# Attention over 48x48 pixels: the softmax sums by 32x32 transposes and row sums instead of matrix products with ones

## The chip, the cores and the metric

One core of a Trainium2 chip. The metric is the device time of one execution in microseconds (us), as a median of several. Engines are named as the profile names them: PE (TensorE), DVE (VectorE), ACT (ScalarE), POOL (GpSimd) and SP (SyncE, which only issues DMAs here). A POOL instruction or a DMA that SP issues runs beside the others; each engine takes its own instructions strictly in order.

## What is computed

Four images of 512 channels and 48x48 = 2304 pixels: group norm over 32 groups, a projection to q, k and v, attention in 8 heads of 64 channels over all pixels, an output projection, and the input added to it.

```python
b, c, hh, ww = x.shape                       # 4, 512, 48, 48
t = hh * ww
d = c // num_heads
hn = _group_norm(x, gn_scale, gn_bias)
qkv = jnp.einsum('oc,bchw->bohw', qkv_w, hn) + qkv_b[None, :, None, None]
qkv = qkv.reshape(b, 3, num_heads, d, t).astype(jnp.float16)
q, k, v = (qkv[:, 0], qkv[:, 1], qkv[:, 2])
scale = jnp.asarray(1.0 / math.sqrt(math.sqrt(d)), dtype=jnp.float16)
w = jnp.einsum('bhct,bhcs->bhts', q * scale, k * scale)
w = jax.nn.softmax(w, axis=-1)
a = jnp.einsum('bhts,bhcs->bhct', w, v).astype(jnp.float32)
out = jnp.einsum('oc,bchw->bohw', proj_w, a.reshape(b, c, hh, ww)) + proj_b[None, :, None, None]
return x + out
```

The softmax needs, for each head and each query pixel, the sum of the exponentials over the 2304 key pixels. The kernel takes the exponentials without subtracting a maximum; it checks afterwards that all sums lie between 256 and 60000, and a slower general path behind a branch runs if one doesn't.

## The kernel before, in words

**Tiling.** The heads are worked on in pairs: 4 images by 4 pairs make 16 groups g. The 2304 queries of a pair are cut into five blocks j, four of 512 and one of 256 queries. A block is worked through in *units*: in one unit PE makes scores for three tiles (`BURST`) of 128 keys by 512 queries by two heads (for the narrow block, two tiles of keys by 256 queries take the place of each), and ACT exponentiates them. A wide block has six units, the narrow one three, a pair 27, the whole stream 432. Keys lie on the partitions, queries along the free dimension.

**One unit.** `scores` (L943) writes three double banks `ps` in PSUM (a pool of three, so a unit uses all of them) and ACT makes three exponentials of 128x1024 from them into `p` (L962), a 16-bit tile from a pool of three. `values` (L965) runs two units behind (`BEHIND = 2`): it multiplies the exponentials with v into the one accumulation bank `av` (L980); after the block's last unit the bank is copied out to `avx` (L989). `add` (L991) runs one unit behind on DVE: it adds the unit's `p` to a running 16-bit sum `acc` of 128x3072 (L1009). The first addition of a block takes the `p` of its first two units, so the first unit's `p` is held until then. After the last unit two more additions of 128x1024 join the three parts of `acc` (L1012).

**From `acc` to the result.** `acc` holds, for each of 128 partitions (keys), 2x512 partial sums. `add_up` (L1015) sums over the partitions on PE, by products with a matrix of ones, into a bank `sl` of the same one-bank pool as `av`; every row of `sl` is the sum. `rows` (L1043) copies it to SBUF on DVE and sends one row per head by DMA to `sums`, spread over 128 partitions; `check_sums` (L1063) compares it with the limits on POOL; `invert` (L1073) takes the reciprocal and writes it to a DRAM row; `spread` (L1084) reads that row back, broadcast over 64 partitions per head, as `ib`; `divide` (L1094) multiplies `avx` by `ib` on POOL. These steps lie in successive units.

**Work beside.** PE also makes q and k (L709), v (L760) and the output projection (L844), in chains that share one PSUM bank `pw`; DVE copies each finished chain out (L719, L768, L871), and only then can the next chain start. These chains are cut into pieces that stand in a list `beside`; `fill(n)` issues in each unit n as many as a credit, counted in units, allows. DVE's statistics and normalization of the next image are `tasks`, let in by `fill` with a `room` in us that is smaller near the end of a block.

**The order.** It is written out by hand; no scheduler changes it. The loop at L1350 issues, for each unit n: the sums of the block that ended three units ago (`add_up`, `rows`), `scores(n)`, `add` for unit n-1, `values` for unit n-2, `check_sums` and `invert` for the block that ended four units ago, `spread` (five), `divide` (six), and `fill(n)`; in the unit with the sums `fill(n)` comes before `values`, so that PE has work while DVE empties `sl`. The last two blocks but one of the stream (`soon`) and the last one go by ways of their own.

Of the kernel before, what the change touches and what calls it, by code (L numbers as in the profile page):

```python
# [26 lines left out]
P = 128  # L27
# [5 lines left out]
BURST = 3  # L33
# [434 lines left out]
def fast_path(  # L468
# [13 lines left out]

    RES = NC
# [93 lines left out]
    fine = const.tile([P, 2 * QB // P], F32, name="fine")  # L577
    nc.gpsimd.memset(fine, 1.0)
# [20 lines left out]
    SQ = 32  # L599
# [332 lines left out]
    open_sums = set()  # L932
# [10 lines left out]
    def scores(u):  # L943
        g, j, k, _ = u
        o, n = QBLOCKS[j]
        per = QB // n
        qt, kt = qk[g]
        pt = ppool.tile([P, BURST, 2, QB], F16, tag="p", name=f"p_{g}_{j}_{k}")
        for r in range(BURST):
            ps = ps_s.tile([P, 2, QB], F32, tag="ps", name=f"ps_{g}_{j}_{k}_{r}")  # L950
            for a in range(per):
                i = (k * BURST + r) * per + a
                for h in range(2):
                    rows = slice(h * D, (h + 1) * D)
                    nc.tensor.matmul(  # L955
                        ps[:, h, a * n : (a + 1) * n],
                        kt[rows, bass.ts(i, P)],
                        qt[rows, o : o + n],
                        start=True,
                        stop=True,  # L960
                    )
            nc.scalar.activation(pt[:, r], ps, AF.Exp)  # L962
        pts[u] = pt

    def values(u):  # L965
# [21 lines left out]
        if last and u is not stream[-1]:  # L987
            avx[g, j] = work.tile([P, QB], F32, tag="avx", name=f"avx_{g}_{j}")
            nc.vector.tensor_copy(avx[g, j][:, :n], av[0][:, :n])  # L989

    def add(u):  # L991
# [18 lines left out]
        if last:  # L1010
            for r in range(1, BURST):
                nc.vector.tensor_tensor(t[:, 0], t[:, 0], t[:, r], ALU.add)  # L1012
            acc[g, j] = [t[:, :1]]

    def add_up(g, j, bank=None, more=False):  # L1015
# [5 lines left out]
        if bank is None:  # L1021
# [4 lines left out]
            for r in range(t.shape[1])  # L1026
# [17 lines left out]
    def rows(g, j, sl):  # L1044

        o, n = QBLOCKS[j]
        sx = work.tile([P, QB], F32, tag="rows", name=f"slx_{g}_{j}")
        nc.vector.tensor_copy(sx[:, :n], sl[:, :n])  # L1048
        sm = small.tile([P, 2, QB // P], F32, tag="sums", name=f"sums_{g}_{j}")
        for h in range(2):  # L1050
            nc.sync.dma_start(sm[:, h, : n // P], sx[h * D : h * D + 1, :n])
        sums[g, j] = sm
        return sx

# [107 lines left out]
    def ready(b, j):  # L1162

        if b < B - 1:
            return BEHIND + 6
        return BEHIND + (4 if j == NQ - 3 else 5)
# [139 lines left out]
    def fill(n):  # L1306
# [5 lines left out]
        if ended(n - 1):  # L1312
            room = 1.1 if idle else 0.0
        elif ended(n - BEHIND - 1):
# [40 lines left out]
    for n in range(end):  # L1355
# [3 lines left out]
        summed = block_at(n - BEHIND - 1)  # L1359
        if summed:  # L1360
            rows(*summed, add_up(*summed))
        wanted(stream[n][0])
        scores(stream[n])
        if n > 0:
            add(stream[n - 1])
        if summed:

            fill(n)
        if n >= BEHIND:
            values(stream[n - BEHIND])  # L1370
        if block_at(n - BEHIND - 2):
            check_sums(*block_at(n - BEHIND - 2))
            invert(*block_at(n - BEHIND - 2))
        if block_at(n - BEHIND - 3):
            spread(*block_at(n - BEHIND - 3))
        if block_at(n - BEHIND - 4):

            divide(*block_at(n - BEHIND - 4))
        if not summed:
            fill(n)  # L1380
# [53 lines left out]
    every = fine.shape[1] + n  # L1434
    fines = work.tile([P, QB], F32, tag="rows", name="fines")[:, :every]
    nc.gpsimd.tensor_scalar(fines[:, :n], inv, 1.0 / SUM_MAX, None, ALU.is_ge)
    ok = work.tile([P, QB], F32, tag="avx", name="ok")[:, :n]
    nc.gpsimd.tensor_scalar(ok, inv, 1.0 / SUM_MIN, None, ALU.is_le)
    nc.gpsimd.tensor_tensor(fines[:, :n], fines[:, :n], ok, ALU.mult)
    nc.gpsimd.tensor_copy(fines[:, n:], fine)  # L1440
# [11 lines left out]
    for i, (evacuate, store) in enumerate(ends_of):  # L1452
        if i == NC:
            nc.vector.tensor_reduce(good, fines, AX.X, ALU.add)  # L1454
# [62 lines left out]
```

## Time and profile before

| | |
|---|---|
| Median of 3 runs | 1613.72 us (1612.02 to 1614.79) |
| The profiled execution: its time / its span | 1614.36 us / 1612.6 us |
| Mean granted TensorE clock | 0.996 |
| Busy: PE, ACT, DVE, POOL | 98%, 79%, 71%, 20% |
| Exponentials (L962), 1296 of 1027 ns | 1234.2 us busy |
| Running sums (L1009), 270 of 1809 ns and 79 of 1749 ns | 626.5 us busy |

The page shows one execution: the span runs from its first to its last instruction. A matmul's busy time overlaps the next one's, so a busy PE is read from the distance between starts and not from the sum of durations. In the timelines below a line gives the start, the time covered, the engine, the line of the kernel, the operation with what it writes and reads, how many instructions are merged (x6), and in brackets the engine's idle time before and what ended it.

### The profile page before, as it was taken

Reading aid. Unit: us, or ns where it says so; the run is one execution under the profiler, and the core shown is the slowest. Engines: PE = TensorE matmul, PEld = TensorE weight load, DVE = VectorE, ACT = ScalarE, POOL = GpSimd, SP = SyncE. Lnnn points to the kernel's source line nnn. Section 1 sums busy time; section 2 is a strip of 40 time slices with the busy share of each in tenths; the row PEclk is TensorE's granted clock in tenths of the full one; section 3 lists DMA queues with packets and bytes.
Section 4 is the critical chain, followed back from the end, with each engine's and each line's share of the span. In section 5 each row is a group of like instructions: output and inputs, shape, how many; then the busy total and the mean of one; then the engine's idle time right before and its main releaser. Section 6 shows DMA issues by size and latency. Waiting matters only on the chain. (4 is left out here: it accounts for less than half of the span.)

```text
span 1612.6 us, 28321 instructions
## 1 busy us (share of the span) xinstructions
PE 1583.4 (98%) x11500; PEld 695.7 (43%) x11500; DVE 1140.2 (71%) x1301; ACT 1268.4 (79%) x1361; POOL 319.4 (20%) x458
## 2 busy tenths in 40 slices
PE   7999999999999999999999999999999999999997
PEld 2533434443333534555333353355533334434554
DVE  6167668866666678986666666788666676667775
ACT  3077777888888888888887888887878888888894
POOL 1001112211121222312111121221212131222222
PEclk9999999999999999999999999999999999999998
DMA  6002020100000023511000002352100000016424
GB/s 212 11 14 67 11 66 22 18 14 11 14 18 14 11 67 119 162 46 30 14 9 18 14 12 63 96 154 80 31 14 11 15 15 18 10 29 183 129 60 133
DMA packets 94897, 82.10 MB, mean 51 GB/s; under 512 B 50853, under 2 KB 60965, under 8 KB 94757
## 3 DMA queue, kind: packets, MB, share of 16 engines
q1 hardware_dynamic: 92724, 78.35, 17.8%
q8 instruction: 92, 1.51, 0.4%
q10 hardware_dynamic: 1904, 1.84, 0.4%
q14 instruction: 49, 0.39, 0.1%
q0 software_dynamic: 128, 0.01, 0.0%
HBM read 60.70 MB, written 19.17 MB: 50 GB/s over the span
## 5 line engine op out<-in xcount | busy, mean ns | idle before, releaser
L962 ACT ACTIVATE p<-ps 128x1024 f16<-128x1024 f32 x1296 | 1234.2, 1027 | 310.7 <-PE ps L955 309.6
L1009 DVE TENSOR_TENSOR acc<-acc,p 128x3072 f16<-128x3072 f16 x270 | 488.3, 1809 | 69.8 <-ACT p L962 69.1
L709 PE MATMUL pqk<-x,wqkv 128*64 128x512 f32 (+1 forms) x2464 | 519.3, 551 | 0.0
L980 PE MATMUL av<-p,v 128*64 128x512 f16 (+1 forms) x2880 | 361.1, 364 | 0.4 <-DVE slx L1048 0.3
L955 PE MATMUL ps<-q,k 64*128 64x512 f16 (+1 forms) x2880 | 356.5, 358 | 1.7 <-ACT p L962 1.4
L760 PE MATMUL pv<-wqkv,x 128*64 128x256 f32 x2304 | 268.6, 380 | 0.0
L709 PEld LDWEIGHTS pqk<-x,wqkv 128*64 128x64 f32 x2464 | 168.8, 137 | 224.4 <-issue 166.8
L1070 POOL TENSOR_SCALAR in<-sums 128x8 f32<-128x8 f32 (+1 forms) x158 | 118.4, 749 | 713.3 <-DMA sums<-slx 706.8
L955 PEld LDWEIGHTS <-k 64*128 64x128 f16 x2880 | 106.3, 94 | 277.6 <-issue 228.7
L980 PEld LDWEIGHTS <-v 128*64 128x64 f16 x2880 | 131.9, 109 | 213.0 <-issue 168.8
L1096 POOL TENSOR_TENSOR att<-avx,ib 128x512 f16<-128x512 f32 (+1 forms) x78 | 117.2, 1502 | 451.1 <-DMA ib<-row 424.8
L760 PEld LDWEIGHTS pv<-wqkv,x 128*64 128x64 f32 x2304 | 160.1, 137 | 92.8 <-issue 4.5
L1009 DVE TENSOR_TENSOR acc<-p,p 128x3072 f16<-128x3072 f16 x79 | 138.2, 1749 | 0.0
L844 PE MATMUL pr<-a,whi 128*128 128x512 f32 (+1 forms) x311 | 122.7, 402 | 4.9 <-DVE q L719 2.3
L1012 DVE TENSOR_TENSOR acc<-acc 128x1024 f16<-128x1024 f16 x156 | 111.8, 716 | 5.4
L844 PE MATMUL pr<-a,wlo 128*128 128x512 f32 (+1 forms) x311 | 114.3, 375 | 0.0
L719 DVE TENSOR_SCALAR q<-pqk,bqkv 128x512 f16<-128x512 f32 (+1 forms) x79 | 54.9, 695 | 80.0 <-PE pqk L709 79.8
L719 DVE TENSOR_SCALAR k<-pqk,bqkv 128x512 f16<-128x512 f32 (+1 forms) x75 | 52.2, 696 | 77.9 <-PE pqk L709 77.9
L768 DVE TENSOR_TENSOR v<-pv,bv 128x512 f16<-128x512 f32 x72 | 49.8, 691 | 80.9 <-PE pv L760 80.8
L989 DVE COPY avx<-av 128x512 f32<-128x512 f32 (+1 forms) x79 | 50.6, 641 | 63.7 <-PE av L980 63.6
L871 DVE SCALAR_TENSOR_TENSOR r<-pr,bproj,r 128x512 f32<-128x512 f32 (+1 forms) x80 | 54.9, 695 | 45.2 <-PE pr L844 44.7
L844 PEld LDWEIGHTS pr<-a,whi 128*128 128x128 f32 x311 | 58.7, 189 | 44.1 <-issue 20.2
(69 smaller groups left out, 456.7 us busy)
## 6 DMA issues: line engine op xcount, KB each, us to landing
r<-x_dram SPq DMA_DIRECT2D x72, 256.0 KB, 3.2
out_dram<-r SPq DMA_DIRECT2D x69, 256.0 KB, 2.2
ib<-row SPq DMA_DIRECT2D x126, 128.0 KB, 3.1
x<-x_dram SPq DMA_DIRECT2D x62, 256.0 KB, 4.1
x<-x_dram SPq DMA_DIRECT2D x16, 128.0 KB, 4.8
sums<-slx SPq DMA_DIRECT2D x128, 2.0 KB, 2.1
ib<-row SPq DMA_DIRECT2D x30, 64.0 KB, 3.1
wqkv<-qkv_wT_dram SPq DMA_DIRECT2D x2, 768.0 KB, 6.9
```

The source lines that it names most:

```text
L709: nc.tensor.matmul(pw[0][lo : lo + D, :n], wqkv[:, c, w0 + lo : w0 + lo + D], hn[b, c, j], start=(c == 0), stop=(c == NC - 1),)
L719: nc.vector.tensor_scalar(qk[g][part][:, o : o + n], pw[0][:, :n], bqkv[:, col : col + 1], SCALE, ALU.add, ALU.mult,)
L760: nc.tensor.matmul(pw[0][lo : lo + D, a, :], hn[b, c, i * P // QB][:, at + lo : at + lo + D], wqkv[:, c, 2 * C + half * C // 2 :][:, : C / ...
L844: nc.tensor.matmul(ps[:, :n], w[:, c, bass.ts(m, P)], at32[b, j, c], start=(i == 0), stop=(i == len(steps) - 1),)
L871: nc.vector.scalar_tensor_tensor(xt[:, i], places[i], bias, xt[:, i], ALU.add, ALU.add)
L955: nc.tensor.matmul(ps[:, h, a * n : (a + 1) * n], kt[rows, bass.ts(i, P)], qt[rows, o : o + n], start=True, stop=True,)
L962: nc.scalar.activation(pt[:, r], ps, AF.Exp)
L980: nc.tensor.matmul(av[0][lo : lo + D, :n], vv[b, pr // 2][:, i, pr % 2 * P + lo : pr % 2 * P + lo + D], pt[:, r, h, a * n : (a + 1) * n], ...
L1009: nc.vector.tensor_tensor(t, before, pt, ALU.add)
L1012: nc.vector.tensor_tensor(t[:, 0], t[:, 0], t[:, r], ALU.add)
L1070: nc.gpsimd.tensor_scalar(t, sm, limit, None, op)
L1096: nc.gpsimd.tensor_tensor(atts[g][:, o : o + n], avx.pop((g, j))[:, :n], ibs.pop((g, j))[:, :n], ALU.mult,)
```

## The change

The sums over the partitions leave PE. After the block's last addition DVE joins one of the two remaining parts and POOL the other (128x1024 each). One unit later `turn` transposes the joined 128x1024 on DVE in squares of 32x32, into a part of `acc` that is free by then; one more unit later `fold` sums each run of 32 along the free dimension on DVE, which leaves 128x32 partial sums, one for each of four groups of 32 keys, and sends the four groups by four DMAs side by side onto 32 partitions (`quarters`). `invert_turned`, two units later, adds the four, takes the reciprocal, transposes the 32x32 result back, writes it by two DMAs to the DRAM row, and does the check of the limits on POOL on 32 partitions. `spread` and `divide` follow as before, one unit later than before each, and what uses the result is set one unit later as well (`ready`). Blocks that end near the end of the last pair (`soon` and the last) keep the products with ones, and both joins on DVE.

The copy of `av` to `avx` moves from DVE to ACT. It stands between the second and the third exponential of the unit (`last_exp`). `fill` always comes after `values` now, and its `room` for DVE tasks is cut in the unit of the turning and in that of the inversion.

```diff
@@ -574,8 +575,12 @@
     nc.gpsimd.memset(ones16, 1.0)
-    fine = const.tile([P, 2 * QB // P], F32, name="fine")
-    nc.gpsimd.memset(fine, 1.0)
+    fines = const.tile([P, 2 * QB // P + SQ], F32, name="fine")
+    fine = fines[:, : 2 * QB // P]
+    fine_turned = fines[:SQ, 2 * QB // P :]
+    nc.gpsimd.memset(fines, 1.0)
+    tinv = const.tile([SQ, SQ], F32, name="tinv")
+    nc.gpsimd.memset(tinv, 1.0)
...
@@ -929,7 +933,8 @@
         tc.mark_branch_hint_location("fallback", taken, engines)
-    open_sums = set()
+    open_sums, joined = set(), set()
+    turned = {}
     av, acc, pts, avx, sums, rowd, ibs = {}, {}, {}, {}, {}, {}, {}
...
@@ -959,8 +964,11 @@
                         stop=True,
                     )
-            nc.scalar.activation(pt[:, r], ps, AF.Exp)
+            exp = lambda r=r, ps=ps: nc.scalar.activation(pt[:, r], ps, AF.Exp)
+            if r < BURST - 1:
+                exp()
         pts[u] = pt
+        return exp
...
@@ -986,7 +994,11 @@
         if last and u is not stream[-1]:
             avx[g, j] = work.tile([P, QB], F32, tag="avx", name=f"avx_{g}_{j}")
-            nc.vector.tensor_copy(avx[g, j][:, :n], av[0][:, :n])
+            nc.scalar.copy(avx[g, j][:, :n], av[0][:, :n])
+
+    def by_turning(g, j):
+
+        return g < NG - 1 or j < NQ - 3
...
@@ -1008,9 +1020,11 @@
         nc.vector.tensor_tensor(t, before, pt, ALU.add)
         if last:
+            shared = by_turning(g, j)
             for r in range(1, BURST):
-                nc.vector.tensor_tensor(t[:, 0], t[:, 0], t[:, r], ALU.add)
-            acc[g, j] = [t[:, :1]]
+                engine = nc.gpsimd if shared and r == BURST - 1 else nc.vector
+                engine.tensor_tensor(t[:, 0], t[:, 0], t[:, r], ALU.add)
+            joined.add((g, j))
...
@@ -1023,7 +1037,7 @@
             (t, r, a)
             for t in acc.pop((g, j))
-            for r in range(t.shape[1])
+            for r in range(1 if (g, j) in joined else t.shape[1])
             for a in range(per)
...
@@ -1052,6 +1066,53 @@
         return sx
+    def turn(g, j):
+
+        t = acc.pop((g, j))[0]
+        turned[g, j] = t[:, 1].rearrange("p h n -> p (h n)")
+        nc.vector.transpose(turned[g, j], t[:, 0].rearrange("p h n -> p (h n)"))
+
+    def fold(g, j):
+
+        part = small.tile([P, SQ], F32, tag="part", name=f"part_{g}_{j}")
+        nc.vector.tensor_reduce(
+            part,
+            turned.pop((g, j)).rearrange("p (c k) -> p c k", k=SQ),
+            AX.X,
+            ALU.add,
+        )
+        quarters = small.tile([SQ, P // SQ, SQ], F32, tag="quarters", name=f"qs_{g}_{j}")
+        for p in range(P // SQ):
+            nc.sync.dma_start(quarters[:, p, :], part[bass.ts(p, SQ), :])
+        sums[g, j] = quarters
+
+    def invert_turned(g, j):
+        n = QBLOCKS[j][1]
+        per, cols = QB // n, n // SQ
+        quarters = sums.pop((g, j))
+        sm = small.tile([SQ, 2, cols], F32, tag="tsum", name=f"tsum_{g}_{j}")
+        nc.vector.tensor_reduce(
+            sm,
+            quarters.rearrange("i p (h a c) -> i h c p a", h=2, a=per),
+            AX.XY,
+            ALU.add,
+        )
+        nc.vector.reciprocal(tinv[:, : 2 * cols], sm.rearrange("i h c -> i (h c)"))
+        back = small.tile([SQ, SQ], F32, tag="tback", name=f"tback_{g}_{j}")
+        nc.vector.transpose(back, tinv)
+        row = dram.tile([2, QB], F32, tag="row", name=f"row_{g}_{j}")
+        for h in range(2):
+            nc.sync.dma_start(
+                row[h, :n].rearrange("(c i) -> c i", i=SQ),
+                back[h * cols : (h + 1) * cols, :],
+            )
+        rowd[g, j] = row
+        ok = fine_turned[:, : 2 * cols].rearrange("p (h c) -> p h c", h=2)
+        for op, limit in ((ALU.is_ge, SUM_MIN), (ALU.is_le, SUM_MAX)):
+            t = small.tile([SQ, 2, cols], F32, tag="tin", name=f"tin_{g}_{j}")
+            nc.gpsimd.tensor_scalar(t, sm, limit, None, op)
+            nc.gpsimd.tensor_tensor(ok, ok, t, ALU.mult)
+
     def divide_here(g, j, source, products, engine):
...
@@ -1162,8 +1223,8 @@
         if b < B - 1:
-            return BEHIND + 6
-        return BEHIND + (4 if j == NQ - 3 else 5)
+            return BEHIND + 7
+        return BEHIND + (4 if j == NQ - 3 else 6)
...
@@ -1309,9 +1370,9 @@
         idle = beside and beside[0][4] and not beside[0][4]()
-        if ended(n - 1):
+        if ended(n - 1) or ended(n - BEHIND - 3):
             room = 1.1 if idle else 0.0
-        elif ended(n - BEHIND - 1):
+        elif ended(n - BEHIND):
             room = 1.1 if idle else 0.5
...
@@ -1356,28 +1417,25 @@
         while loads and loads[0][0] <= n:
             loads.popleft()[1]()
-        summed = block_at(n - BEHIND - 1)
-        if summed:
-            rows(*summed, add_up(*summed))
+        if block_at(n - BEHIND - 1):
+            fold(*block_at(n - BEHIND - 1))
         wanted(stream[n][0])
-        scores(stream[n])
+        last_exp = scores(stream[n])
         if n > 0:
             add(stream[n - 1])
-        if summed:
-
-            fill(n)
         if n >= BEHIND:
             values(stream[n - BEHIND])
-        if block_at(n - BEHIND - 2):
-            check_sums(*block_at(n - BEHIND - 2))
-            invert(*block_at(n - BEHIND - 2))
+        last_exp()
+        if block_at(n - BEHIND):
+            turn(*block_at(n - BEHIND))
         if block_at(n - BEHIND - 3):
-            spread(*block_at(n - BEHIND - 3))
+            invert_turned(*block_at(n - BEHIND - 3))
         if block_at(n - BEHIND - 4):
-
-            divide(*block_at(n - BEHIND - 4))
-        if not summed:
-            fill(n)
+            spread(*block_at(n - BEHIND - 4))
+        if block_at(n - BEHIND - 5):
+
+            divide(*block_at(n - BEHIND - 5))
+        fill(n)
         if n - BEHIND in soon:
```

The hunks left out move the definition of `SQ = 32`, and make the final count of checked values cover the added columns of `fines`.

More of the change, by code (lines that the diff above doesn't have):

```diff
@@ L481, in fast_path @@
     nc = tc.nc
+    SQ = 32
     RES = NC
@@ L594, in fast_path @@
     ALL = range(NC)
-    SQ = 32
     NGROUP = SQ // GROUP
@@ L1432, in fast_path @@
     store()
-    every = fine.shape[1] + n
-    fines = work.tile([P, QB], F32, tag="rows", name="fines")[:, :every]
-    nc.gpsimd.tensor_scalar(fines[:, :n], inv, 1.0 / SUM_MAX, None, ALU.is_ge)
+    every = fines.shape[1] + n
+    found = work.tile([P, QB], F32, tag="rows", name="fines")[:, :every]
+    nc.gpsimd.tensor_scalar(found[:, :n], inv, 1.0 / SUM_MAX, None, ALU.is_ge)
     ok = work.tile([P, QB], F32, tag="avx", name="ok")[:, :n]
     nc.gpsimd.tensor_scalar(ok, inv, 1.0 / SUM_MIN, None, ALU.is_le)
-    nc.gpsimd.tensor_tensor(fines[:, :n], fines[:, :n], ok, ALU.mult)
-    nc.gpsimd.tensor_copy(fines[:, n:], fine)
+    nc.gpsimd.tensor_tensor(found[:, :n], found[:, :n], ok, ALU.mult)
+    nc.gpsimd.tensor_copy(found[:, n:], fines)
     expect_end(kinds.Pool)
@@ L1453, in fast_path @@
         if i == NC:
-            nc.vector.tensor_reduce(good, fines, AX.X, ALU.add)
+            nc.vector.tensor_reduce(good, found, AX.X, ALU.add)
             nc.tensor.matmul(pf, good, ones, start=True, stop=True)
```

## Prediction, made before the changed kernel was run

> **What bounds the kernel now.** I read the page's shares first, then the waits, then one block of the stream engine by engine.
>
> ```profile
> PE 1583.4 (98%) x11500; PEld 695.7 (43%) x11500; DVE 1140.2 (71%) x1301; ACT 1268.4 (79%) x1361; POOL 319.4 (20%) x458
> ```
> ```profile
> ACT p L962 <- PE ps L955: 309.6, 404, 46.1
> DVE acc L1009 <- ACT p L962: 69.1, 87, 1.4
> ```
> ```profile
> L955 PE MATMUL ps<-q,k 64*128 64x512 f16 x2304 | 316.7, 380 | 1.7 <-ACT p L962 1.4 <-DVE v L768 0.3
> L1012 DVE TENSOR_TENSOR acc<-acc 128x1024 f16<-128x1024 f16 x156 | 111.8, 716 | 5.4
> L1439 POOL TENSOR_TENSOR fines<-fines,ok 128x256 f32<-128x256 f32 x1 | 0.7, 740 | 0.1
> L1431 POOL TENSOR_TENSOR r<-beyond,r 128x512 f32<-128x512 f32 x1 | 1.3, 1272 | 3.5 <-ACT beyond L1429 3.5
> L1429 ACT COPY beyond<-held 128x512 f32<-128x512 f32 x1 | 0.6, 587 | 3.4 <-PE held L844 3.4
> ```
>
> ACT waits for PE's scores 404 times; PE waits for ACT 1.4 us in all. So PE sets the pace: time leaves PE's program one for one, and PE must not start to wait. The timelines of PE, ACT and DVE at the end of one wide block show how near it is to waiting.
>
> ```profile
> 432.06 0.82 PE L955 MATMUL ps<-q,k 64*128 64x512 f16 x6
> 435.30 0.82 PE L955 MATMUL ps<-q,k 64*128 64x512 f16 x6
> 438.44 0.38 PE L1032 MATMUL sl<-acc,ones 128*64 128x512 f16 x2
> 438.76 0.82 PE L955 MATMUL ps<-q,k 64*128 64x512 f16 x6
> 442.02 0.82 PE L955 MATMUL ps<-q,k 64*128 64x512 f16 x6
> ```
> ```profile
> 435.73 2.86 ACT L962 ACTIVATE p<-ps 128x1024 f16<-128x1024 f32 x3 [0.38 <-PE ps L955]
> 439.19 2.86 ACT L962 ACTIVATE p<-ps 128x1024 f16<-128x1024 f32 x3 [0.60 <-PE ps L955]
> 442.46 2.86 ACT L962 ACTIVATE p<-ps 128x1024 f16<-128x1024 f32 x3 [0.41 <-PE ps L955]
> ```
> ```profile
> 434.36 1.42 DVE L1012 TENSOR_TENSOR acc<-acc 128x1024 f16<-128x1024 f16 x2
> 437.00 0.69 DVE L989 COPY avx<-av 128x512 f32<-128x512 f32 x1 [1.22 <-PE av L980]
> 438.66 0.75 DVE L719 TENSOR_SCALAR q<-pqk,bqkv 128x512 f16<-128x512 f32 x1 [0.97 <-PE pqk L709]
> 439.33 0.68 DVE L1048 COPY slx<-sl 128x512 f32<-128x512 f32 x1
> 439.92 1.75 DVE L1009 TENSOR_TENSOR acc<-p,p 128x3072 f16<-128x3072 f16 x1
> ```
>
> A unit is 3.24 us on PE (432.06 to 435.30), with ACT at work for 2.86 of it: ACT's slack is 0.38. Many units are such *tight* ones; others hold two pieces of beside work and last about 5 us.
>
> **What the Trainium skill says.** "Perfetto Trace Analysis", Identifying the Most-Contended Engine, warns that matmul busy time misleads because matmuls are pipelined; the trace agrees (380 ns each, yet six scores in 0.82), so I use distances between starts. "VectorE: DVE Perf Modes", The three transpose paths: DVE transposes 32x32 squares only, 311 ns for 128x128 of 16 bits. "Vector Engine (DVE) Microarchitecture Reference", The reshape front-end and per-opcode configuration: one element per cycle and lane. The trace has only small transposes, and they agree (128x64 in 246 ns). "GPSIMD Engine Reference", Specifications: POOL shares SBUF interfaces with DVE and contends with its two-input instructions. The trace agrees: beside POOL's product at 639.19 DVE's addition at 639.52 took 2.56 us instead of 1.75.
>
> **The change part by part.** 77 blocks go the new way, 62 wide and 15 narrow.
>
> *PE: the products with ones go.* The unit that holds them takes 3.46 us (435.30 to 438.76), 0.22 over 3.24, and the next 3.26, where the pieces stand in another order. That is 0.24 a wide block. At a narrow one exponentials start 3.40 apart (467.20 to 470.60) and then 3.27: 0.19. Saved: 62 x 0.24 + 15 x 0.19 = 17.7 us. What is issued beside is counted in units, not in time, so PE's program loses these 184 products and little else.
>
> *ACT: the copy of av.* The copy of L1429, the same shape from PSUM, took 587 ns; instructions in a row overlap by 0.1 on ACT (three exponentials of 1.03 in 2.86), so it pushes the third exponential back by 0.48. The last exponential would end at 435.73 + 2.86 + 0.48 = 439.07. PE's next scores start at 438.54 without the sums, their third pair 0.44 later, at 438.98, and it needs the bank that this exponential frees; with 0.05 for the hand-over PE stands still for 0.14. A narrow copy (some 0.3) fits in the slack. From the starts of exponentials, 48 of the wide blocks are tight there: 48 x 0.14 = 6.7 us. Bounds: 0 (the copy hidden) and 0.3 each, 14 us. ACT regains 0.38 in each later unit. The copy frees av before the next block's first product, two thirds of a unit later.
>
> *DVE and POOL: the new chain.* Off DVE go avx 0.69, slx 0.68, one join 0.72, a small reciprocal 0.2: 2.3 us. New are the transpose, 311 + 896/0.96 = 1244 ns (estimate from the page named; range 1.0 to 2.2, the upper end if 16-bit data went at half rate); the row sum of 1024, from 428 ns for 264 elements (L1454), 428 + 760/0.96 = 1.22 us; and for the inversion a sum of 128 elements, a reciprocal of 32 and a 32x32 transpose, some 0.3 + 0.35 + 0.2. That is 3.3, so DVE gains 1.0 x 77 = 77 us, to 76%. The share is harmless; the order matters. POOL's join has no row of its shape: from 740 ns for 256 and 1272 for 512 elements, 2.08 ns each, 1024 take 1272 + 1065 = 2.34 us. It can't be a gain, since DVE's transpose waits for it; bounds 1.3 (16-bit twice as fast) and 3.3 (beside DVE's additions).
>
> In the block shown: first join done 434.36 + 0.72 = 435.08; POOL 435.16 to 437.50; transpose 437.54 to 438.78. Queued behind it is the copy-out of q, ready at 438.66: 438.78 to 439.53. PE's next chain needs that at about 438.67 + 1.42 = 440.1 (scores and values come first), so it holds. Row sum to 440.75, first addition of the next block to 442.50. That addition frees the `p` that the unit at 442.02 fills: its first exponential, at 442.46 before, would now start at 442.46 - 0.22 + 0.14 = 442.38. It starts 0.17 late; PE waits only from 0.35 late on. So the cover has 0.2 us left, and nothing is lost. Where the copy-out falls ahead of the transpose (the order alternates, as chains have two pieces), the chain ends 0.7 earlier. In DVE's order in the changed kernel, a normalization or a statistic (0.55 to 0.65) stands between transpose and copy-out in four tight blocks, and the first block joins 1.1 late: 4 x 0.5 + 1 = 3 us lost.
>
> *Queues.* SP issues eight DMAs for a block instead of five, about 0.55 each (two `ib` took 1.11): 1.7 us more in some 20, behind which only loads stand. POOL's check keeps four instructions on fewer partitions. The result comes one unit later; its readers are set later too, so I count that at nothing; if the cover at the end failed it would be one unit, 3.2 us.
>
> Sum: 1613.7 - 17.7 + 6.7 + 3 = 1605.7. It is against the profiled execution, 1614.36 (span 1612.6 and 1.8 around it); the median is 0.6 lower, and I start from the median.
>
> **The rivals.**
> *A. The chain overshoots (slower).* POOL's join, transpose and row sum are 4.8 us in a row, with 0.2 to spare. Each 0.1 over costs PE 0.1 in about 20 tight blocks whose copy-out comes after the transpose, and half that in as many more. For it: POOL's products in this kernel average 1640 ns instead of 1272, through DVE's additions. Against: DVE mostly waits idle while POOL joins. It decides from 0.5 over. With POOL at 3.3 and the transpose at 1.5, 1.2 over, less 0.2: 1.0 x 20 + 0.5 x 20 = 30 us: 1636. At the mid, 0.5 over net, 15 us: 1621.
> *B. The copy eats the gain (about the same).* If it delays the exponential by 0.6 with its wait for av, and the chain overshoots by 0.2, PE loses 48 x 0.26 + 4 = 16, and 3 for the tasks: 1613.7 - 17.7 + 19 = 1615. For: slack is 0.38 and the copy 0.48 or more. Against: values end well before ACT gets there.
> *C. All of it is hidden:* 1613.7 - 17.7 = 1596. For: DVE idles in every unit. Against: the copy alone is longer than the slack.
> That PE would not lose its products can't be: they are out of the program.
>
> **How the numbers follow.** Forecast (1600 to 1610) 0.45; C 0.10; B 0.18; A 0.27, mostly near 1621. The range takes in C's end and A's middle: 1596 to 1625. A measurement here tells about 0.2%, 3.2 us, from no change: faster means below 1610.5 and slower above 1617. Faster is the forecast and C, 0.55; B lies in between, 0.17 same; A and B's upper edge 0.28.
>
> **What would show it.** Right: units at block ends of 3.24 without the 0.22; PE's waits for ACT at L955 (1.4 now) up to about 7 to 10 us, most just after the copy; POOL's join near 2.3; transpose near 1.25, row sum 1.2; ACT's first exponential three units into a block late by under 0.35. Wrong: POOL's join over 3, a transpose near 2, exponentials waiting for DVE, or chains (L709, L760, L844) waiting for copy-outs behind the transpose.

## The result: 0.8% slower, and the profile after

| | before | after |
|---|---|---|
| Median | 1614.26 us (1612.02 to 1615.63, 6 runs) | 1626.12 us (1625.79 to 1628.2, 6 runs) |
| Ratio, 95% interval | | 1.0076 [1.0066, 1.0087] |
| Span of the profiled execution | 1612.6 us | 1625.6 us |

The prediction said 1605.7, with a range up to 1625. It missed by 20 us, and on the wrong side.

First the page's shares and the waits of the changed kernel. A line of waits tells who waited for whom: us in total, times, longest.

```profile
PE 1577.1 (97%) x11316; PEld 687.7 (42%) x11316; DVE 1210.9 (74%) x1376; ACT 1297.1 (80%) x1440; POOL 434.0 (27%) x536
```
```profile
DVE acc L1073 <- POOL acc L1026: 108.4, 68, 2.3
...
ACT p L967 <- PE ps L960: 259.2, 305, 45.9
...
ACT p L967 <- DVE acc L1021: 34.6, 34, 1.8
...
PE ps L960 <- ACT p L967: 6.0, 16, 1.0
...
PE pr L848 <- DVE r L875: 5.1, 7, 1.4
...
PE pv L764 <- DVE v L772: 3.3, 3, 1.3
```

PE has 184 products less and is still the busiest engine. It now waits for ACT 6.0 us instead of 1.4, and for copy-outs by DVE (`r`, `v`). ACT waits for PE 50 us less, and 34.6 us for the first addition of a block, the last link of the new chain. DVE waits 1.6 us for POOL's join in 68 of the 77 blocks.

The groups of the new work (count, then busy us and mean ns of one):

```profile
L1026 POOL TENSOR_TENSOR acc<-acc 128x1024 f16<-128x1024 f16 x77 | 163.5, 2124 | 479.3 <-DVE acc L1026 471.9 <-DMA ib<-row 7.4
L1073 DVE STREAM_TRANSPOSE acc<-acc 128x1024 f16<-128x1024 f16 x77 | 95.8, 1244 | 108.4 <-POOL acc L1026 108.4
L1078 DVE TENSOR_REDUCE part<-acc 128x32 f32<-128x1024 f16 x77 | 92.8, 1206 | 0.5
L997 ACT COPY avx<-av 128x512 f32<-128x512 f32 x64 | 38.0, 594 | 0.0
L1094 DVE TENSOR_REDUCE tsum<-qs 32x32 f32<-32x128 f32 x62 | 21.7, 350 | 0.0
L1100 DVE RECIPROCAL tinv<-tsum 32x32 f32<-32x32 f32 x62 | 21.1, 341 | 2.1
```

Each lies within a tenth of the prediction's value (join 2.34, transpose 1.244, row sum 1.22, copy 0.587, reciprocal 0.35), but for the small sum's 350 ns, taken as 0.3. So the miss isn't in a price. Nor is it at an ordinary block end. This is PE, then ACT, at the end of the same wide block as was shown of before:

```profile
441.05 0.82 PE L960 MATMUL ps<-q,k 64*128 64x512 f16 x6
...
444.29 0.98 PE L960 MATMUL ps<-q,k 64*128 64x512 f16 x6
...
447.69 0.60 PE L960 MATMUL ps<-q,k 64*128 64x512 f16 x4
```
```profile
441.48 1.94 ACT L967 ACTIVATE p<-ps 128x1024 f16<-128x1024 f32 x2 [0.39 <-PE ps L960]
443.31 0.59 ACT L997 COPY avx<-av 128x512 f32<-128x512 f32 x1
443.77 3.81 ACT L967 ACTIVATE p<-ps 128x1024 f16<-128x1024 f32 x4
```

The unit that held the products lasts 3.24 (441.05 to 444.29; before, 435.30 to 438.76, it was 3.46). The next unit, the one after the copy, lasts 3.40 (444.29 to 447.69, before 3.26), because ACT runs from the copy into the next unit's exponentials without a pause. The medians over all blocks are nearly the same: 3.46 and 3.28 before, 3.25 and 3.40 after. That is 0.09 us gained per wide block, and the prediction's terms (0.24 less 0.14) give 0.10.

**Where the time goes** is seen from PE's clock: when the first score product of a block starts, after less before, in us. Images take 20 blocks each, and the next image is prepared in part of them.

| first unit of block | 11 | 14 | 21 | 22 | 31 | 34 | 51 | 71 | 80 |
|---|---|---|---|---|---|---|---|---|---|
| before, at us | 277 | 338 | 464 | 483 | 650 | 715 | 1026 | 1403 | 1583 |
| after less before | -0.1 | +5.5 | +5.4 | +6.2 | +5.2 | +11.7 | +10.9 | +10.0 | +12.0 |

In between it gains slowly, as forecast; the end of a tight narrow block (20, in the units of block 21) gives some of that back. The loss comes in two short stretches, 5.6 us within blocks 11 to 13 and 6.5 within 31 to 33, and 2 more after block 71. Blocks 51 to 56, where another image is prepared, come out even (10.9 at blocks 51 and 57), but there the kernel before had lost time itself: DVE's queue waited for a DMA, and PE waited for the copy-out behind it.

```profile
1041.33 0.18 DVE L1077 RECIPROCAL inv<-sums 128x4 f32<-128x4 f32 x1 [2.90 <-DMA sums<-slx]
```
```profile
1043.12 0.50 PE L844 MATMUL pr<-a,whi 128*128 128x512 f32 x1 [2.34 <-DVE q L719]
```
```profile
1044.00:1047.00 3.00, 3.00 (x10) 1.61 (x10) 1.28 (x2) 0.01 (x1) 0.00 (x0) 0.50 0.28 33
```

The last line is a stretch of 3 us. Its columns are the stretch, its length, the busy us of PE, PE's loads, DVE, ACT and POOL, PE's granted clock, the DMA share and GB/s. After the wait the clock was 0.50, for 3.4 us in all. That costs PE some 1.7 us (an estimate, half of 3.4), it came in some executions only, and it shifts every difference behind it. The profiled execution of the changed kernel has no such stretch before 1612 us; where one bears on an experiment, it is named below.

In the first stretch, this is PE in the changed kernel:

```profile
291.67 0.84 PE L988 MATMUL av<-p,v 128*64 128x512 f16 x6
292.44 0.39 PE L960 MATMUL ps<-q,k 64*128 64x512 f16 x2
293.18 0.39 PE L960 MATMUL ps<-q,k 64*128 64x512 f16 x2 [0.35 <-ACT p L967]
294.09 0.39 PE L960 MATMUL ps<-q,k 64*128 64x512 f16 x2 [0.52 <-ACT p L967]
294.42 0.84 PE L988 MATMUL av<-p,v 128*64 128x512 f16 x6
...
297.84 1.79 PE L764 MATMUL pv<-wqkv,x 128*64 128x256 f32 x12
301.10 2.16 PE L764 MATMUL pv<-wqkv,x 128*64 128x256 f32 x18 [1.48 <-DVE x L664]
```

and in the kernel before, in the same units:

```profile
291.85 1.89 PE L760 MATMUL pv<-wqkv,x 128*64 128x256 f32 x16
293.67 0.82 PE L955 MATMUL ps<-q,k 64*128 64x512 f16 x6
...
295.10 1.89 PE L760 MATMUL pv<-wqkv,x 128*64 128x256 f32 x16
```

Before, v chains of the next image stand in these units. After, they are missing: PE has only scores and values and waits for ACT's exponentials. The v chains come two units later, and then PE waits 1.48 us for DVE's normalization of `x` (L664). A unit on PE that carries nothing beside it is time thrown away; the same products lengthen a later unit.

### The profile page after: what moved, and what is told of

The parts are those of the page before. It is cut to its first block, busy times and chain, and to the rows that moved or that the text cites. A ratio compares the mean times of both kernels' runs of the same rounds, so it can differ in the third digit from the quotient of the medians.

```text
span 1625.6 us, 28473 instructions
## 1 busy us (share of the span) xinstructions
PE 1577.1 (97%) x11316; PEld 687.7 (42%) x11316; DVE 1210.9 (74%) x1376; ACT 1297.1 (80%) x1440; POOL 434.0 (27%) x536
## 5 line engine op out<-in xcount | busy, mean ns | idle before, releaser
L1021 DVE TENSOR_TENSOR acc<-acc,p 128x3072 f16<-128x3072 f16 x270 | 475.4, 1761 | 27.9 <-ACT p L967 25.1
L960 PE MATMUL ps<-q,k 64*128 64x512 f16 (+1 forms) x2880 | 366.5, 358 | 6.8 <-ACT p L967 6.0
L1026 POOL TENSOR_TENSOR acc<-acc 128x1024 f16<-128x1024 f16 x77 | 163.5, 2124 | 479.3 <-DVE acc L1026 471.9
L960 PEld LDWEIGHTS <-k 64*128 64x128 f16 x2880 | 112.8, 94 | 328.1 <-issue 277.2
L1113 POOL TENSOR_SCALAR tin<-tsum 32x32 f32<-32x32 f32 (+1 forms) x154 | 74.9, 486 | 505.5 <-DVE tsum L1094 499.3
L988 PEld LDWEIGHTS <-v 128*64 128x64 f16 x2880 | 125.5, 108 | 197.8 <-issue 158.4
L1073 DVE STREAM_TRANSPOSE acc<-acc 128x1024 f16<-128x1024 f16 x77 | 95.8, 1244 | 108.4 <-POOL acc L1026 108.4
L1157 POOL TENSOR_TENSOR att<-avx,ib 128x512 f16<-128x512 f32 (+1 forms) x78 | 98.2, 1259 | 111.8 <-DMA ib<-row 100.1
L1078 DVE TENSOR_REDUCE part<-acc 128x32 f32<-128x1024 f16 x77 | 92.8, 1206 | 0.5
```

Source lines behind the costliest of these rows:

```text
L960: nc.tensor.matmul(ps[:, h, a * n : (a + 1) * n], kt[rows, bass.ts(i, P)], qt[rows, o : o + n], start=True, stop=True,)
L988: nc.tensor.matmul(av[0][lo : lo + D, :n], vv[b, pr // 2][:, i, pr % 2 * P + lo : pr % 2 * P + lo + D], pt[:, r, h, a * n : (a + 1) * n], ...
L1021: nc.vector.tensor_tensor(t, before, pt, ALU.add)
L1026: engine.tensor_tensor(t[:, 0], t[:, 0], t[:, r], ALU.add)
L1073: nc.vector.transpose(turned[g, j], t[:, 0].rearrange("p h n -> p (h n)"))
L1078: nc.vector.tensor_reduce(part, turned.pop((g, j)).rearrange("p (c k) -> p c k", k=SQ), AX.X, ALU.add,)
```

## The experiments

The first theory laid the miss on the changed steps at block ends: the copy on ACT and the inversion. The rival laid it on DVE in the stretches where the next image is prepared, either because `room` holds its tasks back there or because it has no time left. All ratios are against the kernel before, run beside it (median 1614.4 or within 0.3 of it).

**e1_copy_dve** (after, with the copy back on DVE)

```diff
-            nc.scalar.copy(avx[g, j][:, :n], av[0][:, :n])
+            nc.vector.tensor_copy(avx[g, j][:, :n], av[0][:, :n])
```

> The changed kernel with one edit: av is copied to avx by DVE again, not by ACT; the third exponential stays where it is. First theory (ACT's copy pushes the third exponential past its slack, and the traces show the next unit 3.40 us instead of 3.24 at some 45 wide blocks): 45 x 0.14 gives back 6 us, 1620 instead of 1626, since DVE makes the copy in the time in which it waits for POOL. Rival (DVE's order after the block's end is what is too full): the 0.69 us come on top of it, and the time stays at 1626 or rises.

Measured: 1628.68 us, 1.0088 [1.0072, 1.0103]. The units after a wide block are 3.25 now, by the median, so the stall of 0.15 is ACT's copy. But the time didn't fall, it is 2.6 us longer: DVE is busy 1253.7 us instead of 1210.9, and that costs more than the stall did. At the start of block 14 it is 9.1 us behind before, where after is 5.5. The first theory falls here: the copy alone is not what makes the kernel slow. (The run trades the stall for DVE work; e8_copy_third below takes the stall away without it.)

**e2_old_room** (after, with the `room` rule of before)

```diff
-        if ended(n - 1) or ended(n - BEHIND - 3):
+        if ended(n - 1):
             room = 1.1 if idle else 0.0
-        elif ended(n - BEHIND):
+        elif ended(n - BEHIND - 1):
```

> The changed kernel with one edit: the room that DVE's tasks get in each unit is that of the kernel before (none in the first unit after a block's end, 0.5 in the third, 1.1 otherwise). First theory (the smaller room delays the next image's normalization, v chains that wait for it are held back, two units run without beside work, and later units wait for DVE; 5 us are lost in one place near 290 us and perhaps as much at later images): 1616 to 1621. Rival (the room only shifts tasks; what is lost is lost to the longer chain of join, transpose and row sum): tasks now fall between transpose and copy-out, and the time is 1626 or more.

Measured: 1620.52, 1.0033 [1.002, 1.0045]: 5.6 us come back. Of the loss in blocks 11 to 13 only 1.5 is left (0.7 behind before at block 11, 2.2 at block 14). The one in 31 to 33 stays, 6.8 us; some 1.7 of that is the clock in this execution, 0.5 for 3.4 us from 675.3 on, after PE had waited 2.16 for DVE's `r`.

**e3_invert_later** (after, with inversion, spread, division and `ready` one unit later)

```diff
-        if block_at(n - BEHIND - 3):
-            invert_turned(*block_at(n - BEHIND - 3))
         if block_at(n - BEHIND - 4):
-            spread(*block_at(n - BEHIND - 4))
+            invert_turned(*block_at(n - BEHIND - 4))
...
```

> The changed kernel with one edit: the inversion, the spreading and the division of a block each come one unit later, and their readers too. In the changed kernel the inversion of the block before falls into the same unit as the transpose of the narrow block, ahead of a copy-out of a q or k chain. First theory (this puts 0.9 us between transpose and copy-out at narrow blocks, and PE loses some 0.7 us at 8 to 10 of them): 6 us back, 1620. Rival (that order costs nothing because narrow blocks have their own slack): 1626.

Measured: 1625.04, 1.0065 [1.0051, 1.0078]: 1.1 us by the medians, 2.9 by the spans (1622.7 for 1625.6), less than expected. What it cures is seen in DVE's timeline of the changed kernel at a narrow block:

```profile
474.56 1.25 DVE L1073 STREAM_TRANSPOSE acc<-acc 128x1024 f16<-128x1024 f16 x1 [2.30 <-POOL acc L1026]
475.73 0.32 DVE L1094 TENSOR_REDUCE tsum<-qs 32x32 f32<-32x128 f32 x1
476.09 0.34 DVE L1100 RECIPROCAL tinv<-tsum 32x32 f32<-32x32 f32 x1
476.46 0.20 DVE L1102 STREAM_TRANSPOSE tback<-tinv 32x32 f32<-32x32 f32 x1
476.60 0.70 DVE L723 TENSOR_SCALAR k<-pqk,bqkv 128x512 f16<-128x512 f32 x1
477.23 1.20 DVE L1078 TENSOR_REDUCE part<-acc 128x32 f32<-128x1024 f16 x1
478.53 1.76 DVE L1021 TENSOR_TENSOR acc<-p,p 128x3072 f16<-128x3072 f16 x1
```

A narrow block has three units, so the inversion of the block before it falls into the unit of its own transpose, and 0.9 us stand ahead of the copy-out of k at 476.60. PE's next chain waits 0.39 for it at 477.35, and ACT's exponential at 480.38 waits 1.72 for the addition. The third and the fifth unit after a narrow block last 3.70 and 3.49 for 3.25, by the median (3.85 and 3.64 after the block shown); with the inversion one unit later both are 3.25.

**e4_join_dve** (after, with both joins on DVE)

```diff
-                engine = nc.gpsimd if shared and r == BURST - 1 else nc.vector
+                engine = nc.vector
```

> The changed kernel with one edit: DVE makes both joins, POOL none, and the transpose need not wait for POOL (DVE stands waiting for it 108 us in all). First theory (several causes, of which the long chain is one): the chain ends 1.4 us earlier, which takes away the losses at narrow blocks and part of those in the stages with tasks, but neither the copy's nor the held v chains': 1614 to 1619. Rival (the chain through POOL is the whole cause): all of the loss goes and the products' gain comes out, about 1600. Second rival (DVE has no room for it): 1626 or more.

Measured: 1625.05, 1.0066 [1.0052, 1.0079]. DVE is busy 1300.6 us instead of 1210.9 (80% of the span), and the kernel isn't slower for it. DVE's wait for POOL is gone, and so is the pile at narrow blocks (3.25 by the median). In blocks 31 to 33 it loses 5.3 instead of 6.5. There DVE of the changed kernel waited for POOL's join three times, 3.7 us in all, and three joins of its own are 2.1 us of work: in that stretch POOL's join takes nothing off DVE.

**e5_norm_pool** (after, with the normalization of `x` on POOL)

```diff
-        nc.vector.tensor_scalar(t, t, ga, gb, ALU.mult, ALU.add)
+        nc.gpsimd.tensor_scalar(t, t, ga, gb, ALU.mult, ALU.add)
```

> The changed kernel with one edit: POOL, not DVE, normalizes the later images' x (60 instructions of some 0.53 us, all in the stretches in which the next image is prepared). First theory (in those stretches DVE was over 0.9 busy before the change, and the 1 us that it gains per block makes it the bound there): 30 us off DVE just there give back 5 to 8 us, 1618 to 1621. Rival (there the loss comes from the order in which chains are held back and issued, not from DVE's load): POOL normalizes no earlier, and the time is 1626 or more.

Measured: 1627.93, 1.0085 [1.0071, 1.0099], no gain. In POOL's queue the second normalization stands behind a check of the limits and starts at 301.80, on DVE in the changed kernel at 298.0; PE waits 4.29 us for `x` instead of 1.48, and the clock is 0.5 for 6.8 us there. Between blocks 12 and 14 it loses 10.2 us, after 7.2. So this run doesn't show what relief for DVE would be worth.

**e8_copy_third** (after, with all three exponentials ahead of ACT's copy)

```diff
-            if r < BURST - 1:
-                exp()
+            exp()
         pts[u] = pt
-        return exp
+        return lambda: None
```

> The changed kernel with one edit: ACT's copy of av comes behind the unit's third exponential instead of ahead of it. First theory (the copy stops PE because it delays the exponential whose bank PE needs for the next unit's third pair of scores; behind it, it only shifts the next unit's first exponential by about 0.1, inside the slack): units after a wide block 3.25 instead of 3.40, 45 x 0.15 = 7 us back, 1619. Rival (0.48 us of work for ACT in a unit with 0.38 of slack cost the same wherever they stand): 1626.

Measured: 1623.01, 1.0053 [1.0039, 1.0067]: 3.1 us less than after, half of what the prediction's 6.7 for the copy would give back. The wide units are 3.25 after a block's end.

**e6_before_copy_act** (before, with ACT's copy alone, where the change has it)

```diff
-            nc.vector.tensor_copy(avx[g, j][:, :n], av[0][:, :n])
+            nc.scalar.copy(avx[g, j][:, :n], av[0][:, :n])
...
```

> The kernel before with one part of the change: ACT copies av to avx, between the second and the third exponential, and everything else stays. First theory (the products with ones stand 0.22 us ahead of the next scores on PE, which covers the 0.14 by which the copy is late): 1612 to 1614, the same as before or slightly faster, since DVE loses 50 us of work. Rival (the copy costs 0.14 at each tight wide block whatever stands on PE): 1621.

Measured: 1615.98 (21 runs), 1.0011 [1.0004, 1.0018]. The copy costs nearly nothing in the kernel before: its units are 3.46 and 3.28 as without it. In the unit where the products with ones stand PE comes 0.22 later, and that covers the copy. It costs only once the products are gone, so the prediction was right to price the two in one unit.

**e7_before_new_room** (before, with the changed `room` alone)

```diff
-        if ended(n - 1):
+        if ended(n - 1) or ended(n - BEHIND - 3):
             room = 1.1 if idle else 0.0
-        elif ended(n - BEHIND - 1):
+        elif ended(n - BEHIND):
```

> The kernel before with one part of the change: the smaller room for DVE's tasks (none in the first and the fifth unit after a block's end, 0.5 in the second). First theory (the smaller room by itself delays the normalization and holds v chains back near 290 us): 1617 to 1620. Rival (it does so only together with the longer work of DVE at a block's end): 1614, the same.

Measured: 1623.26, 1.0056 [1.0042, 1.007]: this edit alone loses 8.8 us, with no new instruction on any engine. PE in this kernel, in the units shown above:

```profile
291.78 0.39 PE L955 MATMUL ps<-q,k 64*128 64x512 f16 x2
292.70 0.39 PE L955 MATMUL ps<-q,k 64*128 64x512 f16 x2 [0.52 <-ACT p L962]
293.61 0.39 PE L955 MATMUL ps<-q,k 64*128 64x512 f16 x2 [0.52 <-ACT p L962]
```

It is the same picture: units with no v chain in them, at ACT's pace. With less room for tasks the normalization comes later: the first one starts at 292.7 here and at 294.4 in the changed kernel, but at 282.4 in the kernel before and at 285.6 in e2_old_room. v chains aren't issued until their `x` is normalized, and `beside` is taken in order, so what stands behind them waits too. It loses 5.3 us between blocks 12 and 14, 3.3 from block 11 on. Of the rest, 2.3 lie in blocks 31 to 33 and 3.0 in 51 to 56, where PE stood still for 3.98 us (before 2.34) and the clock was 0.5 for 6.8 us (before 3.4); that the edit causes this wait isn't shown.

**e11_before_more_dve** (before, with one more DVE transpose of 128x1024 at each of 77 blocks; nothing reads its result)

```diff
+        if block_at(n - BEHIND):
+            t = whole.pop(block_at(n - BEHIND))
+            nc.vector.transpose(
+                t[:, 1].rearrange("p h n -> p (h n)"),
+                t[:, 0].rearrange("p h n -> p (h n)"),
+            )
...
```

> The kernel before with nothing of the change but DVE's load: at 77 blocks DVE also transposes the joined 128x1024 into a part of the sum that is free, and nobody reads it (1.24 us each, in the second unit after a block's end). First theory (in the stretches with statistics, normalization and projection DVE is over 0.9 busy, so more work there is paid in full, and elsewhere not at all): 1.2 us at 6 to 8 blocks, 1620 to 1624. Rival (DVE's load is harmless, what costs is the waiting for POOL and the room): 1614 to 1616.

Measured: 1621.58, 1.0039 [1.0025, 1.0052] by the ratio of runs side by side. 77 x 1.24 = 95.8 us of DVE work cost some 6 to 7 us. In the profiled execution, 1618.56, PE falls back 1.0 us before block 12, 1.7 in blocks 29 to 33 and 2.4 in 51 to 56 (some 4 if the stretch of half clock that the kernel before had there is left out), and hardly elsewhere. The busy times of two stretches show why (columns as above); first before, then this kernel:

```profile
338.00:463.00 125.00, 125.00 (x880) 46.94 (x880) 84.43 (x85) 102.56 (x109) 19.11 (x31) 1.00 0.06 13
...
640.00:695.00 55.00, 54.63 (x352) 30.66 (x350) 50.12 (x73) 45.50 (x53) 17.34 (x25) 1.00 0.55 156
```
```profile
643.00:698.00 55.00, 53.97 (x351) 29.65 (x349) 52.04 (x77) 43.87 (x52) 16.73 (x24) 1.00 0.52 150
```

DVE is busy 84 of 125 us (68%) in a quiet stretch, where the extra transposes are free, and 50 of 55 (91%) where statistics, normalization and the output projection's copy-outs fall together. The 71% of the page is the mean over all stretches and lies between the two.

**e10_mixed** (after, with the old `room`, and the new way only in blocks that end with no task pending: 58 turn, 19, nearly all of them in blocks 8 to 12, 27 to 32 and 48 to 54, use the products with ones in the order of before)

```diff
-        return g < NG - 1 or j < NQ - 3
+        if (g, j) not in ways:
+            ways[g, j] = (g < NG - 1 or j < NQ - 3) and not tasks
+        return ways[g, j]
...
```

> The changed kernel, but a block's sums are taken by transposes only if no task of the next image (statistics, normalization) is pending when the block ends: 58 blocks turn, 19 take the products with ones in the order of the kernel before (both joins on DVE, chains between scores and values); the room is that of the kernel before. ACT copies av between the second and third exponential in all. First theory (the loss lies in the stretches with tasks, by the smaller room and by DVE's load, and there it now goes away; elsewhere the copy gives back 0.15 of the 0.24 and the inversion at narrow blocks costs 0.7): 1611 to 1615, the time of the kernel before. Rival (the turning costs everywhere): 1620 or more.

Measured: 1614.62, 0.9998 [0.9989, 1.0006]: 5.9 us better than e2_old_room, which turns all blocks. Blocks 31 to 33 lose 1.3 instead of 6.8 (some 5.1 without that run's stretch of half clock).

**e9_mixed_best** (e10_mixed, with ACT's copy behind the third exponential in turned blocks and on DVE in the others, and the inversion one unit later)

```diff
-            nc.scalar.copy(avx[g, j][:, :n], av[0][:, :n])
+            if by_turning(g, j):
+                nc.scalar.copy(avx[g, j][:, :n], av[0][:, :n])
+            else:
+                nc.vector.tensor_copy(avx[g, j][:, :n], av[0][:, :n])
...
```

> As the mixed kernel (58 blocks by transposes, 19 by products with ones), and all the causes found so far taken away: ACT copies behind the third exponential in turned blocks, DVE copies in the others, and the inversion of a turned block comes one unit later. First theory: of the 1614.4 of the kernel before, 58 blocks save 0.2 to 0.24 each and nothing comes back: 1600 to 1604. Rival (some cost of the turning is still unknown): 1608 or more.

Measured: 1603.03 (1601.71 to 1603.54), 0.9925 [0.9911, 0.9938]: faster than both kernels. By the medians it is 11.3 us ahead of before, in the profiled execution 12.9 at block 80. The prediction's saving for 58 blocks is 58 x 17.7 / 77 = 13.3, so where DVE has time, nearly all of it arrives. The waits of this kernel:

```profile
DVE acc L1078 <- POOL acc L1031: 77.5, 52, 2.3
...
PE ps L960 <- ACT p L967: 1.8, 4, 0.5
```

PE's waits for ACT are back at 1.8 us, and DVE's wait for POOL is still there, 1.5 us in 52 of the 58 turned blocks: in the quiet stretches it is harmless.

**e12_mended** (after, with the three repairs of e2, e3 and e8 together, all 77 blocks turned; it differs from e9_mixed_best in the 19 blocks)

> The changed kernel with three edits together and every block turned as in the change: the room of the kernel before, ACT's copy behind the third exponential, and the inversion one unit later. First theory (what is left over the mixed kernel's 1603 is DVE's load in the stretches with tasks): their single gains of 5.6, 3.1 and 1.1 add up, 1614 to 1617, some 12 us above the mixed kernel. Rival (the three are the whole cause, and turning in the stretches with tasks costs nothing by itself): 1600 to 1606.

Measured: 1615.37 (21 runs), 1.0006 [0.9999, 1.0012]. Between the stretches it gains as e9_mixed_best does (5.8 us from block 34 to 71, there 7.5), but it loses 2.5 in blocks 11 to 13, 5.8 in 31 to 33 and 3.3 from 73 to 77. By the medians the two kernels are 12.3 us apart. In the profiled executions it is 14.0 at block 80: 9.3 up to block 73 (e9 had a stretch of half clock of its own there, 3.4 us from 1036.5), and 4.8 in blocks 73 to 77, all of which both kernels turn. There PE of e12 waited for POOL's conversion of `a`, and then the clock was 0.5 for 3.4 us:

```profile
1475.25 0.51 PE L848 MATMUL pr<-a,whi 128*128 128x512 f32 x1 [2.15 <-POOL a L840]
```

So not all of the distance is the 19 blocks' own. In blocks 31 to 33 (no such stretch of the clock) PE waits for copy-outs of the output projection, and DVE's timeline shows what these wait behind; the line of waits is for 620 to 720 us:

```profile
PE pr L848 <- DVE r L875: 4.9, 6, 1.4
```
```profile
655.41 1.25 DVE L1072 STREAM_TRANSPOSE acc<-acc 128x1024 f16<-128x1024 f16 x1 [1.65 <-POOL acc L1025]
656.58 0.71 DVE L612 BATCH_NORM_STATS2 st<-x 128x6 f32<-128x256 f32 x2
657.20 0.74 DVE L875 SCALAR_TENSOR_TENSOR r<-pr,bproj,r 128x512 f32<-128x512 f32 x1
657.86 1.21 DVE L1077 TENSOR_REDUCE part<-acc 128x32 f32<-128x1024 f16 x1
659.17 1.76 DVE L1020 TENSOR_TENSOR acc<-p,p 128x3072 f16<-128x3072 f16 x1
660.85 0.35 DVE L1093 TENSOR_REDUCE tsum<-qs 32x32 f32<-32x128 f32 x1
661.24 0.34 DVE L1099 RECIPROCAL tinv<-tsum 32x32 f32<-32x32 f32 x1
661.61 0.20 DVE L1101 STREAM_TRANSPOSE tback<-tinv 32x32 f32<-32x32 f32 x1
661.75 0.37 DVE L612 BATCH_NORM_STATS2 st<-x 128x6 f32<-128x256 f32 x1
662.05 0.72 DVE L875 SCALAR_TENSOR_TENSOR r<-pr,bproj,r 128x512 f32<-128x512 f32 x1
```

From 655.41 on DVE doesn't stop, beyond the end of these lines. The chain whose copy-out starts at 662.05 holds PE's one bank for beside work, and PE stood still for 1.27 us before its next product at 662.91. Just before these lines DVE itself had waited 1.65 us for POOL, longer than the wait it then caused.

## Why the prediction was wrong, step by step

**The step that failed first** is "What is issued beside is counted in units, not in time, so PE's program loses these 184 products and little else". The count stays, but what may be issued depends on `x` being normalized, and the change's own edit of `room` puts that off. The diff showed the edit and the prediction gave it no price. It costs 8.8 us alone (e7, where the held chains are shown for blocks 11 to 13 and the rest isn't traced to them), 5.6 in the changed kernel (e2). Most of the first stretch of the table is this.

**The second** is "so DVE gains 1.0 x 77 = 77 us, to 76%. The share is harmless". The sum is right: DVE's busy time rose by 70.7 us. The share was read from the page, as a mean over stages. In the stretches where the next image is prepared (91% in the one shown) PE pays for the added work: 6 to 7 us in e11, where nothing but DVE work was added. Between e12 and e9 it is 12.3 us by the medians, some 9 of 14 in the traces; this takes in the wait for POOL, and the two kernels also differ in who copies `av` in the 19 blocks and in where `fill` stands. The prediction's "3 us" for tasks between transpose and copy-out came nearest to this mechanism, mis-sized: it counted single tasks at four tight blocks, not a queue that stays full for three blocks. The profile before held a sign of it, PE's wait of 2.34 us for DVE's `q` shown above; the prediction read only PE's waits for ACT. The Trainium skill says in "Perfetto Trace Analysis", Optimization Strategy, that some kernels have several regimes, with another engine the most contended in each. The traces agree in part: DVE's share is 68% in one of the stretches shown and 91% in the other, but PE has the highest share in both, and DVE as the second one decides what an addition costs.

**Omitted**: at a narrow block the previous block's inversion falls between transpose and copy-out (0.45 + 0.24 us a tight narrow block; 1.1 us by the medians and 2.9 by the spans, e3). Counting units would have shown it: the inversion comes three units after the transpose of its block, and a narrow block has three.

**Right**: the saving of the products, 0.24 a tight wide block (3.46 + 3.28 became 3.25 + 3.25 in e8, and e9 cashes it), and by PE's starts the same 0.24 at a tight narrow one, for which the prediction had read 0.19 from exponentials; the copy's stall, 0.15 measured for 0.14, though taking it away gave back 3.1 us and not 6.7 (e8); the durations; the result one unit later at nothing (e3 and e9 put it off by one more and lose nothing by it); the first block, 0.8 us lost in the second block's units for 1 forecast.

**The rivals.** Rival A forecast a loss in the same place, the chain of join, transpose and row sum, but by longer durations ("It decides from 0.5 over"). These were not over; POOL's join was 0.2 under. Its number for the mid case, 1621, was nearer, but by luck, for another reason. Of the prediction's signs of being wrong two came, exponentials that wait for DVE (34.6 us) and chains that wait for copy-outs (`r` 5.1, `v` 3.3); the two long durations named with them did not.

**The sum.** From after, the three repairs take 10.8 us off (e12: 1615.4; one by one 5.6 + 1.1 + 3.1 = 9.8), and e9, which differs in the 19 blocks, 12.3 more (1603.0). The parts don't simply add: e10 gains 5.9 over e2 from the 19 blocks, and the copy and the inversion are worth 11.6 between e10 and e9, but 5.2 between e2 and e12. These compare medians, and some of it may lie in how the copy is done in the 19 blocks, which changed with them; no run takes that apart.

**Open.** PE once waits 1.54 us in the changed kernel (at 675.97) for POOL's conversion of `a`, which stands behind a product that waits for `ib`; no run takes that alone away (in e12 the wait there is 0.4, and blocks 31 to 33 still lose 5.8). The same kind of wait, 2.15 us, is at the root of e12's loss from block 73 on; why e9 has none there stays open. Nor was the loss in the second stretch split further between DVE's added work and its wait for POOL: e4 trades one for the other and gains 1.2 us there.

## What to carry to other kernels

Before an engine's extra load is called harmless, cut the span into stages and read its share in each: 71% on average was 91% where it mattered, and in that stage both its work and its waits in an in-order queue came out of the bound engine's time. An edit that only holds work back (a budget, a due time) has a price of its own; ask which later work is gated by what is held back, and what the bound engine does meanwhile. Read the granted clock of each stretch before two traces are compared: a few us at half clock were as large as some of the differences here. And a new step may be right in most of a stream and wrong in a stage: using it only where there is room turned a loss of 0.8% into a gain of 0.75%.

## What the runs showed of the hardware

- DVE transposed 128x1024 of 16 bits in squares of 32x32 in 1244 ns, as the prediction's estimate had it; the same elements' row sum took 1206 ns and their addition 704.
- POOL added 128x1024 of 16 bits in 2124 ns, 2.07 ns an element, three times DVE's; 16 bits gave it nothing over the slope of 2.08 ns between the 32-bit rows of the kernel before.
- DVE's reciprocal on 32 partitions took 341 ns for 32 columns and 241 for 16, so 6.2 ns a column, against about 1.2 ns an element of the transpose.
- ACT's copy of 594 ns from PSUM put the next exponential back by only 0.46 us (443.31 to 443.77).
- Short POOL instructions stretched beside DVE's additions: the check of the limits, 0.28 us by itself, took 1.71 at 434.90, beside an addition that began at 434.70.
- In the stream (up to 1590 us) PE stood still for 1.97 to 4.29 us ten times in these profiles. In seven its granted clock was 0.5 for 3.4 or 6.8 us, beginning during or just after the wait (before 2.34, e2 2.16, e5 4.29, e7 3.98, e9 1.97, e10 2.00, e12 2.15); in three it was not (e3 2.23, e4 2.06, e11 2.32). After shorter waits, up to 1.90 us, there was none.
